# Softmax totals spread through DRAM, and one sequence's layernorm moved into the sequence before

## The chip, the cores and the metric

The kernel runs on one core of one Trainium2 chip. Its time is device microseconds for one execution. All data are float32.

## What is computed

There are four sequences of 1024 tokens with 1024 features. Each passes through a causal attention layer of 32 heads of 32 features, and then through a layer in which each token uses the best of 8 low-rank adapters. Both layers have a layernorm without weights before them and a residual around them.

```
xn   = layernorm(x)                                  # (4, 1024, 1024)
q,k,v = xn @ wq, xn @ wk, xn @ wv                    # 32 heads x 32
q, k = rotary(q), rotary(k)
p    = softmax(causal(q k^T / sqrt(32)))             # per head 1024 x 1024
x    = x + (p v) @ wo
y    = layernorm(x)
gate = one_hot(argmax(y @ route_w^T)) * max(y @ route_w^T)      # of 8
x    = x + ((gate * (y @ A^T)) @ Bw) * scaling       # rank 16 each
```

## The kernel before

**Units.** A unit is one sequence `b` with one group `g` of four heads; there are 32 units, `units[u]`, in order of sequence, so units 0 to 7 are sequence 0. In each unit the kernel scores four heads, exponentiates, and multiplies with the values. Queries come as 16 tiles `t` of 64; a "half" `blk` is eight of these tiles. Beside that, between the scores of unit `u`, a list of steps `between[u]` is worked off: the projections `q`, `k`, `v` for unit `u + 1` (`chain`, 8 matmul steps for each of 6 chains, L302), and from sequence 1 on a part of the *previous* sequence's end: one token tile of `wo` (`project`), its layernorm and transposes (`turn`), the router (`route`), and the adapter (`turn_hidden`, `adapt`).

**The order.** All engines' queues are in the order in which the program text is run; nothing is reordered later. A unit runs through eleven `SLOTS`. Most are score rounds: `score_round` (TensorE, then copies by ScalarE, then the mask by GpSimd at L420), `find_tops` (VectorE's row maxima, L438, and their exchange, L459), some exponentials (ScalarE, L467), whose 32x32 transposes by VectorE (`turn_probabilities`, L492) make them ready for the value matmuls. After each round `fill` works off a share of the steps, by their costs (a projection step is 1.0; steps of cost 0 only put an instruction in its place). The two slots `"second"` and `"first"` call `apply`, which multiplies one half with the values (`value_pieces`, L573, for the second half of unit `u - 1` and the first half of unit `u`), and then scales the result by the reciprocal of the softmax totals (`scale_values`, L593). Until L593 has read it, the bank of the value sums is not free for the next score round.

**The totals.** `join_sums` adds the two halves of the totals (L534), takes the reciprocal on VectorE (L535), and lets GpSimd copy each reciprocal 32 times (L537) into a tile `by` of queries by features. `spread_sums` turns `by` to features by queries with four transposes on TensorE (L547) and one copy by ScalarE (L548). L593 multiplies with it. `join_sums` is called as soon as the last tile of a half has been transposed; `spread_sums` behind the value matmuls.

**Postponed work.** `postponed` holds pairs of a cost and a function. After each step `do_postponed` takes the step's cost off and runs what has come down to zero. It serves the rotary embedding.

**The next sequence's layernorm.** `Norm` does it for a sequence's eight token tiles: `load` (a DMA from `x` to a tile of tag `row`, of which there are five, or to a tile of a not yet used `qT` or `kT`, as `homes` says), `find` (moments, L175 to L181), `scale` (L186), and `turn` (eight transposes on TensorE, L198, and two copies). `after` names the tiles that are loaded when one has been turned. For sequence 1, the loads of tiles 0 to 4 stand at the start of unit 5's steps; two tiles are scaled in unit 5, four in unit 6, and the last two in unit 7. Tiles 0 to 3 can only be turned when the projections of unit 7 have released the old `xnT`, in unit 6; the others are turned in unit 7, by the list that `change_steps` builds. For sequences 2 and 3 `change_steps` also weaves in what the previous sequence has left: `p` (16 `wo` steps), `tail` (`turn`, `route`, `turn_hidden`, `adapt`) and `held`, the last value chain of the unit, as `h[0]` to `h[7]`.

**Streams.** SyncE's queue (SP) issues all DMAs. From sequence 1 on the `wo` and router weights come as chunks in four tiles of tag `chunk` (`load_chunk`, L647); the chunk four places on is loaded when one has been used. The values go through DRAM as well (`vd`, L507 and L513).

Of the kernel before, what the change touches and what calls it, by code (L numbers as in the profile page):

```python
# [14 lines left out]
P = 128  # L15
# [56 lines left out]
def tile_preln_attn_then_top1_lora(  # L72
# [87 lines left out]
    half_sb = const.tile([P, 1], F32, name="half_sb")  # L160
    nc.vector.memset(half_sb, -0.5)
    sign_sb = const.tile([P, 1], F32, name="sign_sb")

    def sign_sines():

# [60 lines left out]
    def do_postponed(cost):  # L226
        for item in list(postponed):
            item[0] -= cost
            if item[0] <= 0:
                postponed.remove(item)  # L230
                item[1]()

    class Norm:

# [8 lines left out]
        def load(self, *tiles):  # L245
            u = self.b * NG
            for t in tiles:
                n = self.homes.get(t)
                if not n:
                    self.x[t] = load_x(self.b, t)  # L250
                    continue
                dsts = qTs if n == "q" else kTs
                if u not in dsts:
                    dsts[u] = big.tile([P, S], F32, tag="qkT", name=f"{n}T_{u}", bufs=4)
                self.x[t] = dsts[u]
                nc.sync.dma_start(dsts[u], x[self.b, t * P : (t + 1) * P, :])
# [7 lines left out]
        def scale(self, t):  # L264
            while self.scaled <= t:
                k = self.scaled
                self.find(k + 1 if self.b == 0 else k)
                normalize(self.x[k], self.x[k], self.moments.pop(k))
                self.scaled += 1
                if self.b == 1:  # L270
                    self.find(k + 1)

        def turn(self, t):
            half, k = divmod(t, TB)
# [250 lines left out]
    def join_sums(u, blk):  # L525


        if (u, blk) in bys or any((u, t) in places for t in range(blk * QT, (blk + 1) * QT)):
            return
        den = dens.pop((u, blk)).rearrange("p (t c) h -> p c t h", c=2)  # L530
        rec = small.tile([P, TB, HG], F32, tag="rec", name=f"rec_{u}_{blk}", bufs=2)
        for i in range(P // SQ):
            rows, other = slice(i * SQ, (i + 1) * SQ), slice((i ^ 1) * SQ, ((i ^ 1) + 1) * SQ)
            nc.vector.tensor_tensor(rec[rows], den[rows, i % 2], den[other, i % 2], ALU.add)  # L534
        nc.vector.reciprocal(rec, rec)  # L535
        bys[u, blk] = by = big.tile([P, TB, P], F32, tag="by", name=f"by_{u}_{blk}")
        nc.gpsimd.tensor_copy(  # L537
            by.rearrange("p t (h d) -> p t h d", d=HD),
            rec.unsqueeze(3).to_broadcast([P, TB, HG, HD]),
        )  # L540

    def spread_sums(u, blk):

        by = bys.pop((u, blk))
        pt = bank([P, TB, P], f"pr_{u}_{blk}")
        for i in range(TB):
            nc.tensor.transpose(pt[:, i, :], by[:, i, :], eye_sb)  # L547
        nc.scalar.copy(by, pt)  # L548
        return by.rearrange("p t k -> p (t k)")

    def value_pieces(u, blk):

# [236 lines left out]
    def change_steps(u, norm, project, tail, held):  # L789
# [7 lines left out]
        if p:  # L797
            turn, route, turn_hidden, adapt = tail
            find = norm.finding
            load_last = Step(lambda: norm.load(7), 0.0)  # L800
            out += [*h[:2], turn, *h[2:4], find(3), p[0], h[4], turning(2), h[5], p[1], route, scaling(3)]
            out += [find(4), h[6], p[2], h[7], p[3], turn_hidden, scaling(4), *p[4:6], adapt, load_last]
            out += [p[6], find(5), p[7], turning(3), scaling(5), *p[8:10], turning(4), *p[10:12]]
            chains = weave(chains[:-6], p[12:]) + chains[-6:]
            out += [*chains[:2], find(6), *chains[2:4], scaling(6), turning(5), *chains[4:6], find(7)]
            out += [*chains[6:8], scaling(7), turning(6), *chains[8:14], turning(7)]
            return out + chains[14:]
        out += [*chains[:2], turning(4), scaling(6), *chains[2:6], turning(5), scaling(7)]
        out += [*chains[6:11], turning(6), *chains[11:16], turning(7)]
        return out + chains[16:]  # L810

    USUAL = (("q", 0), ("k", 0), ("q", 1), ("k", 1), ("v", 0), ("v", 1))
    ENDING = (("q", 0), ("q", 1), ("k", 0), ("v", 0), ("k", 1), ("v", 1))
# [8 lines left out]
    for u, (b, g) in enumerate(units):  # L822
# [13 lines left out]
        if u + 1 < len(units) and g + 1 == NG:  # L836
            last_v = between[-1]
            if b:
                norm = Norm(b + 1, {0: (2,), 2: (5,), 3: (6,)}, {3: "q", 4: "k", 6: "q"})
                load = [Step(lambda norm=norm, t=t: norm.load(t), 0.0) for t in range(2)]  # L840
                for at, step in (
                    (own["k", 0][0], load[0]),
# [9 lines left out]
                ):  # L852
                    behind(last_v, at, step)
            else:
                norm = Norm(b + 1, {0: (5,), 1: (6,), 2: (7,)})
                for t, at in enumerate((("k", 1), ("k", 1), ("k", 1), ("v", 1))):
                    behind(last_v, own[at][(1 + 3 * t) % NC], norm.turning(t))
                behind(last_v, own["v", 1][6], norm.scaling(5))
                behind(last_v, own["v", 1][3], norm.finding(5))
                behind(last_v, own["k", 0][4], norm.scaling(4))  # L860
                behind(last_v, own["q", 1][2], norm.scaling(3))
                behind(last_v, own["q", 0][2], norm.scaling(2))
                for t in (1, 0):
                    between[-2].insert(10 + 16 * t, norm.scaling(t))
                between[-2].insert(0, Step(lambda norm=norm: norm.load(*range(TB + 1)), 0.0))
            steps = change_steps(u + 1, norm, project, tail, held)
            norms[b + 1] = norm
        else:
# [274 lines left out]
```

## Time and profile before

| What | us |
|---|---|
| median of 3 runs (lowest, highest) | 2747.32 (2746.83, 2750.49) |
| the profiled execution: own time | 2747.7 |
| its span | 2745.9 |
| one unit of sequence 0 (unit 3) | 65.3 |
| units 5, 6, 7, in which sequence 1 is normalized | 70.2, 77.5, 72.8 |
| one steady unit of sequences 1 to 3 | 82.3 |
| units 15 and 23, in which the sequence changes later | 97.7 |

A unit is measured here from its first value matmuls for the second half of the unit before it to the same place in the next unit. In the profile, L12 is line 12 of the kernel; PE is TensorE, PEld its weight loads, DVE VectorE, ACT ScalarE, POOL GpSimd, SP SyncE. A group's line gives the busy time, the mean duration of one in ns, and the idle time of that engine just before it with what ended it. A line of the timeline gives start and length in us, engine, line, operation, what is written and read, and in brackets the idle time before. Two records belong to each float32 matmul step of 512 columns.

### The profile page before, as it was taken

The page shows a single profiled execution, that of the slowest core. Times are in us where ns is not written, and L with a number is a line of the kernel's source. Part 1 is how long each engine was busy: PE and PEld are TensorE (multiplying, and loading weights), DVE is VectorE, ACT ScalarE, POOL GpSimd, SP SyncE. Part 2 cuts the span into 40 slices and gives each one's busy share as a digit, 9 for nine tenths or more (in the row PEclk, how much of TensorE's full clock was granted, in tenths as well). Part 3 has the DMA queues.
Part 4 walks back from the last instruction along what each step waited for, and adds up shares of the span by engine and source line. Part 5 has one row for each costly group of instructions (what it writes and reads, how often), then busy time and mean ns, then how long its engine had stood idle before and what let it go on. Part 6 is the DMA issues. An engine that isn't in the chain of part 4 may idle for free.

```text
span 2745.9 us, 84082 instructions
## 1 busy us (share of the span) xinstructions
PE 2682.2 (98%) x35328; PEld 1322.0 (48%) x35328; DVE 2126.7 (77%) x4198; ACT 1755.0 (64%) x5033; POOL 638.1 (23%) x900
## 2 busy tenths in 40 slices
PE   8999999899999999989999999998999999999998
PEld 5444444444445444445444454444544444544445
DVE  4888889887777877887777778788777777778655
ACT  2877777876666676666666666666566666666521
POOL 2222223222222222222222222222222222222000
PEclk9999999999999999999999999999999999999999
DMA  3222232325444455551654444565255544446421
GB/s 118 52 56 56 56 94 56 78 56 150 131 135 114 121 141 142 151 171 43 175 145 122 135 110 121 149 165 146 63 157 150 138 128 128 115 119 196 129 67 55
DMA packets 448012, 317.86 MB, mean 116 GB/s; under 512 B 150289, under 2 KB 371729, under 8 KB 447633
## 3 DMA queue, kind: packets, MB, share of 16 engines
q1 hardware_dynamic: 447632, 312.47, 41.6%
q8 instruction: 278, 4.55, 0.7%
q14 instruction: 102, 0.83, 0.1%
HBM read 262.59 MB, written 49.81 MB: 114 GB/s over the span
## 4 chain that ended last, share of the span: by engine, by line
PE 80%; DVE 14%; ACT 2%; DMA 1%; POOL 1%; issue 1%; SPq 0%; POOLq 0%; DVEq 0%; ACTq 0%
PE po L690 14%; PE pq L313 14%; PE pk L313 13%; PE pv L313 12%; PE s L406 11%; PE av L573 9%; DVE top L438 4%; DVE pr L492 4%; PE ph L712 2%; PE pf L751 2%; DMA chunk<-in_wo 1%; DVE both L459 1%; PE pr L547 1%; ACT pr L417 1%; PE pt_f L198 1%
## 5 line engine op out<-in xcount | busy, mean ns | idle before, releaser
L467 ACT ACTIVATE pr<-pr,both 128x256 f32<-128x256 f32 (+15 forms) x2048 | 1045.1, 519 | 58.0 <-DVE both L459 57.9
L438 DVE TENSOR_REDUCE top<-pr 128x2 f32<-128x960 f32 (+15 forms) x768 | 651.1, 894 | 251.5 <-POOL pr L420 250.9
L417 ACT COPY pr<-s 128x640 f32<-128x640 f32 (+14 forms) x544 | 525.3, 1017 | 492.3 <-PE s L406 491.7
L492 DVE STREAM_TRANSPOSE pr<-pr 128x1024 f32<-128x1024 f32 (+11 forms) x768 | 664.3, 907 | 33.3 <-ACT pr L467 30.1
L420 POOL TENSOR_TENSOR pr<-pr,causal_sb 128x128 f32<-128x128 f32 x512 | 238.0, 472 | 1070.6 <-ACT pr L417 1062.4
L313 PE MATMUL pv<-xnT,wv 128*128 128x512 f32 x1024 | 484.1, 600 | 0.0
L313 PE MATMUL pq<-xnT,wq 128*128 128x512 f32 x1008 | 476.8, 600 | 0.6 <-ACT xnT L200 0.6
L313 PE MATMUL pk<-xnT,wk 128*128 128x512 f32 x1008 | 475.9, 601 | 0.0
L406 PE MATMUL s<-kT,qT 32*32 32x256 f32 (+4 forms) x17408 | 393.0, 385 | 10.7 <-ACT pr L417 7.2
L467 ACT ACTIVATION_READ_ACCUMULATOR pr<-pr,both 128x1 f32 x2048 | 400.8, 196 | 0.0
L690 PE MATMUL po<-chunk,attn 128*128 128x512 f32 x736 | 376.3, 597 | 4.0 <-DMA chunk<-in_wo 4.0
L406 PEld LDWEIGHTS s<-kT,qT 32*32 32x32 f32 x17408 | 187.2, 103 | 267.2 <-issue 101.8
L313 PEld LDWEIGHTS pk<-xnT,wk 128*128 128x128 f32 x1008 | 181.3, 190 | 234.8 <-issue 234.6
L313 PEld LDWEIGHTS pq<-xnT,wq 128*128 128x128 f32 x1008 | 182.6, 191 | 224.0 <-issue 221.8
L313 PEld LDWEIGHTS pv<-xnT,wv 128*128 128x128 f32 x1024 | 185.7, 190 | 217.2 <-issue 212.9
L573 PE MATMUL av<-pr,vals 64*32 64x256 f32 (+3 forms) x12288 | 273.2, 320 | 11.7 <-DVE pr L492 11.6
L573 PEld LDWEIGHTS av<-pr,vals 64*32 64x32 f32 x12288 | 215.5, 106 | 119.9 <-issue 54.5
L459 DVE TENSOR_TENSOR both<-top 32x4 f32<-32x4 f32 (+3 forms) x1152 | 213.4, 185 | 23.7
L690 PEld LDWEIGHTS po<-chunk,attn 128*128 128x128 f32 x736 | 135.2, 190 | 168.0 <-issue 149.6
L548 ACT COPY by<-pr 128x512 f32<-128x512 f32 x64 | 37.5, 586 | 260.5 <-PE pr L547 260.5
L593 DVE TENSOR_TENSOR at<-av,by 128x256 f32<-128x256 f32 x128 | 48.1, 417 | 158.1 <-ACT by L548 158.0
L690 PE MATMUL po<-wo,attn 128*128 128x512 f32 x256 | 116.7, 597 | 0.0
(87 smaller groups left out, 1705.8 us busy)
## 6 DMA issues: line engine op xcount, KB each, us to landing
chunk<-in_wo SPq DMA_DIRECT2D x368, 256.0 KB, 3.6
vals<-vd SPq DMA_DIRECT2D x256, 128.0 KB, 4.5
x<-in_x SPq DMA_DIRECT2D x58, 512.0 KB, 6.0
wq<-in_wq SPq DMA_DIRECT2D x32, 512.0 KB, 4.0
wk<-in_wk SPq DMA_DIRECT2D x32, 512.0 KB, 4.0
wv<-in_wv SPq DMA_DIRECT2D x32, 512.0 KB, 4.2
vd<-vT SPq DMA_DIRECT2D x128, 128.0 KB, 4.8
out_y<-x SPq DMA_DIRECT2D x32, 512.0 KB, 2.8
```

What stands on the lines that cost most here:

```text
L313: nc.tensor.matmul(at["p"], lhsT=wt[:, c, :], rhs=xnTs[b, tb][:, c, :], start=(c == 0), stop=(c == NC - 1),)
L406: nc.tensor.matmul(sc[i * SQ : (i + 1) * SQ, h, at : at + w].rearrange("p (j k) -> p j k", k=SQ), lhsT=of_q[rows, 2 * t + half], rhs=of_k[ ...
L417: nc.scalar.copy(pr[:, :, k0 : k0 + w], sc[:, :, at : at + w])
L420: nc.gpsimd.tensor_tensor(diagonal, diagonal, causal_sb.unsqueeze(1).to_broadcast([P, HG, SQ]), ALU.add)
L438: nc.vector.tensor_reduce(top[:, k, h : h + step], places[u, t][:, h : h + step, :], AX.X, ALU.max, negate=True,)
L459: nc.vector.tensor_tensor(dst[rows], src[rows], src[other], op)
L467: nc.scalar.activation(pr[:, h, :], pr[:, h, :], AF.Exp, bias=tops[u, t][:, h : h + 1], accum_out=dens[u, t // QT][:, t % QT, h : h + 1],)
L492: nc.vector.transpose(pr, pr)
L573: nc.tensor.matmul(avs[half][h * HD : (h + 1) * HD, t0:, :], lhsT=v[rows, j, h * HD : (h + 1) * HD], rhs=rhs, start=(j == 0), stop=(j == n ...
L690: nc.tensor.matmul(st["po"], lhsT=lhsT, rhs=rhs, start=(c == start), stop=(c == stop))
L712: nc.tensor.matmul(ph, lhsT=st["ynT"][:, c, :], rhs=w[:, c - i * RA, :], start=(c == 0), stop=(c == NC - 1),)
L751: nc.tensor.matmul(pf, lhsT=st["whT"], rhs=rhs, start=True, stop=True)
```

## The change

1. `join_sums` no longer uses GpSimd. The reciprocals lie as 16 columns (head by tile) in a constant tile `rec_sb`, are transposed in 32x32 blocks on VectorE, and go to DRAM by four small DMAs (`put`); four more (`get`) read them back, each row of 512 totals to the 32 partitions of its head. In sequence 0 both are issued at once; later `put` and `get` are postponed by costs of 2.0 and 4.0. `spread_sums` issues what is still left and returns `by`; its transposes and its copy are gone.
2. Sequence 1's tiles 0 to 3 are loaded, measured and scaled one per unit in units 1 to 4, tiles 4 and 5 in unit 5, tiles 6 and 7 in unit 6. Tiles 5 and 6 lie in two `chunk` tiles each (`Two` hides that from the readers), and are scaled in two instructions of 512 columns.
3. `change_steps` takes its steps in another order. With a previous sequence to finish, all of `h` comes ahead of the second `wo` step, and tile 6 is loaded in a `row` together with tile 7, behind `adapt`, and no longer in `qT` when tile 3 has been turned. Without one, the tiles are turned after 3, 4, 4 and 4 steps.

```diff
+    rec_sb = const.tile([P, 2, SQ], F32, name="rec_sb")
+    nc.vector.memset(rec_sb, 0.0)
...
+                if n == "chunk":
+                    self.x[t] = Two([])
+                    for cols in (slice(0, HALF), slice(HALF, D)):
+                        part = big.tile([P, HALF], F32, tag="chunk", name=f"x_{self.b}_{t}", bufs=4)
+                        nc.sync.dma_start(part, x[self.b, t * P : (t + 1) * P, cols])
+                        self.x[t].parts.append(part)
+                    continue
...
-                normalize(self.x[k], self.x[k], self.moments.pop(k))
+                moments = self.moments.pop(k)
+                for part in getattr(self.x[k], "parts", [self.x[k]]):
+                    normalize(part, part, moments)
                 self.scaled += 1
-                if self.b == 1:
-                    self.find(k + 1)
...
-        den = dens.pop((u, blk)).rearrange("p (t c) h -> p c t h", c=2)
-        rec = small.tile([P, TB, HG], F32, tag="rec", name=f"rec_{u}_{blk}", bufs=2)
+        den = dens.pop((u, blk)).rearrange("p (t c) h -> p c h t", c=2)
+        rec = rec_sb[:, blk, : HG * TB].rearrange("p (h t) -> p h t", t=TB)
         for i in range(P // SQ):
             rows, other = slice(i * SQ, (i + 1) * SQ), slice((i ^ 1) * SQ, ((i ^ 1) + 1) * SQ)
             nc.vector.tensor_tensor(rec[rows], den[rows, i % 2], den[other, i % 2], ALU.add)
-        nc.vector.reciprocal(rec, rec)
-        bys[u, blk] = by = big.tile([P, TB, P], F32, tag="by", name=f"by_{u}_{blk}")
-        nc.gpsimd.tensor_copy(
-            by.rearrange("p t (h d) -> p t h d", d=HD),
-            rec.unsqueeze(3).to_broadcast([P, TB, HG, HD]),
-        )
+        nc.vector.reciprocal(rec_sb[:, blk, : HG * TB], rec_sb[:, blk, : HG * TB])
+        turned = small.tile([P, SQ], F32, tag="recT", name=f"recT_{u}_{blk}", bufs=2)
+        nc.vector.transpose(turned, rec_sb[:, blk])
+        there = dram.tile([HG * TB, P // SQ, SQ], F32, tag="recs", name=f"recs_{u}_{blk}")
+        by = big.tile([P, TB * P], F32, tag="by", name=f"by_{u}_{blk}")
+
+        def put():
+            for i in range(P // SQ):
+                nc.sync.dma_start(there[:, i], turned[i * SQ : i * SQ + HG * TB])
+
+        def get():
+            for h in range(HG):
+                of_h = there[h * TB : (h + 1) * TB]
+                nc.sync.dma_start(
+                    by[h * HD : (h + 1) * HD],
+                    bass.AP(of_h.tensor, of_h.offset, [[0, HD], [1, TB * P]]),
+                )
+
+        left = [put, get]
+        bys[u, blk] = by, left
+        for cost in (2.0, 4.0) if units[u][0] else (0.0, 0.0):
+            postponed.append([cost, lambda: left and left.pop(0)()])
+        do_postponed(0.0)
...
-        by = bys.pop((u, blk))
-        pt = bank([P, TB, P], f"pr_{u}_{blk}")
-        for i in range(TB):
-            nc.tensor.transpose(pt[:, i, :], by[:, i, :], eye_sb)
-        nc.scalar.copy(by, pt)
-        return by.rearrange("p t k -> p (t k)")
+        by, left = bys.pop((u, blk))
+        while left:
+            left.pop(0)()
+        return by
...
-            load_last = Step(lambda: norm.load(7), 0.0)
-            out += [*h[:2], turn, *h[2:4], find(3), p[0], h[4], turning(2), h[5], p[1], route, scaling(3)]
-            out += [find(4), h[6], p[2], h[7], p[3], turn_hidden, scaling(4), *p[4:6], adapt, load_last]
-            out += [p[6], find(5), p[7], turning(3), scaling(5), *p[8:10], turning(4), *p[10:12]]
+            load_last = Step(lambda: norm.load(6, 7), 0.0)
+            out += [*h[:2], turn, *h[2:4], find(3), *h[4:8], p[0], turning(2), p[1], scaling(3), p[2]]
+            out += [route, find(4), *p[3:5], turn_hidden, scaling(4), p[5], adapt, load_last, p[6]]
+            out += [find(5), p[7], turning(3), scaling(5), *p[8:10], turning(4), *p[10:12]]
             chains = weave(chains[:-6], p[12:]) + chains[-6:]
-            out += [*chains[:2], find(6), *chains[2:4], scaling(6), turning(5), *chains[4:6], find(7)]
-            out += [*chains[6:8], scaling(7), turning(6), *chains[8:14], turning(7)]
+            out += [*chains[:2], find(6), *chains[2:4], turning(5), scaling(6), *chains[4:7], find(7)]
+            out += [*chains[7:9], turning(6), scaling(7), *chains[9:14], turning(7)]
             return out + chains[14:]
-        out += [*chains[:2], turning(4), scaling(6), *chains[2:6], turning(5), scaling(7)]
-        out += [*chains[6:11], turning(6), *chains[11:16], turning(7)]
-        return out + chains[16:]
+        for t, n in zip(range(TB, NT), (3, 4, 4, 4)):
+            out += [*chains[:n], turning(t)]
+            del chains[:n]
+        return out + chains
...
-                norm = Norm(b + 1, {0: (2,), 2: (5,), 3: (6,)}, {3: "q", 4: "k", 6: "q"})
+                norm = Norm(b + 1, {0: (2,), 2: (5,)}, {3: "q", 4: "k"})
...
-                norm = Norm(b + 1, {0: (5,), 1: (6,), 2: (7,)})
+                norm = Norm(b + 1, {0: (7,)}, {5: "chunk", 6: "chunk"})
+                for t, (unit, at) in enumerate(((1, 24), (2, 24), (3, 24), (4, 24), (5, 12), (5, 36))):
+                    steps = between[unit]
+                    for k, step in enumerate((norm.load, norm.find, norm.scale)):
+                        steps.insert(at - 8 + 5 * k, Step(lambda step=step, t=t: step(t), 0.0))
+                for at, step in (
+                    (own["q", 0][0], Step(lambda norm=norm: norm.load(6), 0.0)),
+                    (own["q", 1][0], norm.finding(6)),
+                    (own["q", 1][3], norm.scaling(6)),
+                    (own["v", 1][5], norm.finding(7)),
+                    (own["v", 1][7], norm.scaling(7)),
+                ):
+                    behind(last_v, at, step)
                 for t, at in enumerate((("k", 1), ("k", 1), ("k", 1), ("v", 1))):
                     behind(last_v, own[at][(1 + 3 * t) % NC], norm.turning(t))
-                behind(last_v, own["v", 1][6], norm.scaling(5))
-                behind(last_v, own["v", 1][3], norm.finding(5))
-                behind(last_v, own["k", 0][4], norm.scaling(4))
-                behind(last_v, own["q", 1][2], norm.scaling(3))
-                behind(last_v, own["q", 0][2], norm.scaling(2))
-                for t in (1, 0):
-                    between[-2].insert(10 + 16 * t, norm.scaling(t))
-                between[-2].insert(0, Step(lambda norm=norm: norm.load(*range(TB + 1)), 0.0))
```

More of the change, by code (lines that the diff above doesn't have):

```diff
@@ L231, in do_postponed, with __init__, __getitem__ @@
                 item[1]()
+    class Two:
+        def __init__(self, parts):
+            self.parts = parts
+        def __getitem__(self, key):
+            rows, cols = key
+            k, at = divmod(cols.start, HALF)
+            return self.parts[k][rows, at : at + cols.stop - cols.start]
     class Norm:
```

## The prediction

> **What bounds it now.** I read the busy shares and the chain of waits first, then the stage table, then the spots that the diff touches.
>
> ```profile
> PE 2682.2 (98%) x35328; PEld 1322.0 (48%) x35328; DVE 2126.7 (77%) x4198; ACT 1755.0 (64%) x5033; POOL 638.1 (23%) x900
> PE 80%; DVE 14%; ACT 2%; DMA 1%; POOL 1%; issue 1%; SPq 0%; POOLq 0%; DVEq 0%; ACTq 0%
> ```
>
> TensorE (PE) is nearly always busy and holds most of the chain; VectorE (DVE) holds 14% of it. Where that share lies, the stage table shows for one unit of sequence 1 (first line) and one of sequence 0 (second line; a unit's time runs from the first value matmuls for the second half of the unit before to the same place one unit on; columns: window, length, busy us of PE, weight loads, DVE, ACT, POOL, then clock, DMA share, GB/s):
>
> ```profile
> 1374.55:1456.87 82.32, 82.32 (x1094) 40.04 (x1093) 64.22 (x127) 53.66 (x157) 19.48 (x28) 1.00 0.47 130
> 269.85:335.14 65.29, 64.37 (x1033) 30.61 (x1032) 56.48 (x112) 52.46 (x154) 18.46 (x26) 1.00 0.25 59
> ```
>
> From sequence 1 on PE has no gap in a steady unit, and DVE has 18 us to spare: PE time taken out there shortens the run one to one. In sequence 0 a unit has no `wo` projection; DVE is 56.5 of 65.3 us busy and PE already waits 0.9 us in it. The largest waits of PE:
>
> ```profile
> PE av L573 <- DVE pr L492: 11.6, 2, 9.1
> PE pt_a L198 <- ACT yn L200: 5.2, 2, 2.6
> PE pt_a L198 <- DVE qT L186: 4.5, 2, 2.3
> PE po L690 <- DMA chunk<-in_wo: 4.0, 5, 1.7
> ```
>
> The 9.1 us lie at 539 to 548, in unit 6, where DVE normalizes four tiles of sequence 1; the next two are at the later changes of sequence (1185 and 1229, again 1860 and 1904). The change meets both. Its other part removes these:
>
> ```profile
> L547 PE MATMUL pr<-eye_sb,by 128*128 128x128 f32 x256 | 42.2, 287 | 0.9 <-issue 0.9
> L548 ACT COPY by<-pr 128x512 f32<-128x512 f32 x64 | 37.5, 586 | 260.5 <-PE pr L547 260.5
> L537 POOL COPY by<-rec 128x512 f32<-128x512 f32 x64 | 39.1, 612 | 220.1 <-DVE rec L535 220.1
> ```
>
> **What the Trainium skill says.** "DMA: Bandwidth & Descriptors", Anatomy of one DMA, gives some 2.0 us fixed per DMA, mostly the receipt of the last write. It is fitted on GpSimd's path; here the 256 KB `attn<-at` stores from SP land after 3.4 us and the 128 KB `vals<-vd` loads after 4.5, so 2 us for a few KB is plausible. The same page, Rules for kernel authors, has the issuing engine wait for a first DMA before a second reads what it wrote: each `get` waits on SP for its `put`, as `vals<-vd` does now behind `vd<-vT` (33.2 us of SP waits in 33). "TensorE: Matmul & The Clock Gate", Part 1, halves PE's clock after some 3.4 us idle: after the 9.05 us wait the 128 value matmuls take 5.90 us, elsewhere 3.68.
>
> **The change, part by part.** *PE.* Four transposes stand together 64 times. The timeline of one:
>
> ```profile
> 708.01 0.66 PE L547 MATMUL pr<-eye_sb,by 128*128 128x128 f32 x4
> 708.50 1.02 PE L690 MATMUL po<-chunk,attn 128*128 128x512 f32 x2
> ```
>
> The next matmul starts 0.49 us after them, not 287 ns times four: that is what they hold. 64 x 0.49 = 31.4 us in all. *ACT* loses 64 x 0.586 us and a wait in its queue for PE; it is not the bound. *POOL* loses 64 x 0.61, and one thing on DVE's path:
>
> ```profile
> 303.76 0.61 POOL L537 COPY by<-rec 128x512 f32<-128x512 f32 x1 [5.24 <-DVE rec L535]
> 304.33 0.46 POOL L420 TENSOR_TENSOR pr<-pr,causal_sb 128x128 f32<-128x128 f32 x1
> 304.82 1.09 DVE L438 TENSOR_REDUCE top<-pr 128x2 f32<-128x896 f32 x1 [1.19 <-POOL pr L420]
> ```
>
> The mask addition (its input is there at 301.3) stands behind the copy, which stands behind the reciprocal; DVE idles 1.19 us. That goes, once per unit. *DVE* gains a 128x32 transpose; the 128x128 one takes 0.30 us, I take 0.2 (0.1 to 0.3).
>
> *The way by DRAM.* From the reciprocal's start: 0.25 and 0.2 us on DVE; four stores issued at 0.35 each on SP (`attn<-at` takes 0.33), 1.4; landing 2.0; four loads issued, 1.4; landing 2.1. Sum 7.4 us. Bounds: 5.5, were issue 0.1 each; 14.2 with the landings of `vd<-vT` (4.8) and `vals<-vd` (4.5) and 0.75 per store. By now L593 comes at least 7.9 us after the reciprocal in sequence 0 (first half of the queries), 9.3 there (second half), some 10.8 later, but 3.0 in unit 0. L593 could come 1.3 us sooner where it waits for ACT. In sequence 1, window 9.4: hidden; the `put` and `get` come up to 4 units of cost later in SP's order, still ahead of L593, and the next scores need the bank only 4 us after it. In sequence 0, first half, DVE loses its 1.19 of idle, so the window is 6.7: L593 waits 0.7. In unit 0 it waits about 4.4 us, ahead of a PE wait for DVE (2.6 us at 135) that has no slack.
>
> *SP behind the put.* `put` waits for DVE, `get` for the landing; chunk loads of `wo` and the router stand behind. At the second half of unit 10 SP would be held from about 861 to 868; the chunk issued at 864.1 is used at 875.4, with 7.5 us to spare after landing (3.9 us). Hidden, at some 3 us left. If the way takes 14 us, it is about 1 us late per unit.
>
> *Normalization, sequence 0.* One tile is 2 x 0.68 + 0.21 + 0.15 + 0.81 = 2.53 us of DVE. Before: tiles 0 and 1 in unit 5, four tiles in unit 6, the rest in 7. Now one tile in each of units 1 to 4, two in 5, two in 6, none in 7. The new loads stand 10 us ahead of their use, on an SP that is idle there (x lands in 6.0).
> - Units 1 to 4: PE from the values to tile 15's scores 17.5 - 0.5 = 17.0; ACT and POOL 4.7; DVE from 292.06 to 334.70 with no gap but the 1.19, 42.6 - 1.2 + 2.5 + 0.2 + 0.7 = 44.9; hand-over 0.4. That is 67.1 against 65.3, so +1.8; PE alone would allow -1.9. I take +1.5 each, +6 (from -8 to +10).
> - Unit 0: +4.4 (0 to +6). Unit 5: from 70.2 to some 67.7, -2.5.
> - Unit 6: between 514.6 and 548.6 DVE does three moment findings and two scalings, 7.4 us with a wait for POOL; now one tile, 3.2. L593 comes about 1.8 sooner. The values then start some 6 us earlier, -6; what is late next is still DVE, by some 3 us, so I give no cold clock back.
> - Unit 7: -1.0 on PE, and less DVE: -1.5.
> Sequence 0 together: +4.4 + 6 - 2.5 - 6 - 1.5 = **+0.4**. The cut there is spent on the spread tiles.
>
> *Steady units of sequences 1 to 3* (19 of them, and unit 31): 20 x 0.98 = **-19.6**.
>
> *The two later changes of sequence* (units 14 with 15, and 22 with 23). Tile 6 loaded with tile 7, not after tile 3: the 2.3 us go. Three steps of the held value chain moved ahead of tile 2: the 2.6 us for `yn` go at that place, but DVE is busy, but for 0.7 us, from 1155 to the values at 1194, so PE meets the wait there; DVE itself gains 1.2 from POOL. Half of the transposes, 1.0, count. Loads of tiles 6 and 7 together put one on SP behind the landing of `out_y` (2.8 us), ahead of the chunk that is already 1.6 late: +1.5. So -1.0 - 2.3 - 1.2 + 1.5 = -3.0 each, **-6**. The other moved steps keep their engines' order within a slot; I cost them at nothing, under DVE's queue; uncovered, 1 us.
>
> Sum: -19.6 - 6 + 0.4 = -25.2. The profiled execution took 2747.7 us (span 2745.9), 0.4 above the median of 2747.32: 2747.7 - 25.2 = 2722.5, **2722**.
>
> **The rivals.**
> - *DVE has room in sequence 0 and the boundary waits go whole.* For it: DVE is 87% busy, not 100. Against: it is without a gap from 292 to 335. Units 0 to 7 then give 0 - 4 - 4 - 9 - 3 = -20, the boundaries 2 x -7.3: 2747.7 - 19.6 - 20 - 14.6 = 2693.
> - *Slower: the way by DRAM is longer than its window.* Place: L593 of the first half in sequence 0, in DVE's gapless stretch. Each us above 7.4 costs 8 units 1 us; from 7.4 + 25.2/8 = 10.5 us on the whole gain is lost. At 12 us: -25.2 + 37 = +12, 2760. For it: landings of 4.5 and 4.8 us in this trace; against: those move 128 KB in small pieces, these 64 KB in rows of 2 KB.
> - *Given back in the steady units*: SP held at `put`, a chunk 1 us late in each of 24 units: +24, 2746, no change. Against: the spare 7.5 us.
> - *The DMAs are only issued at L593*, because the postponed steps have not run: would show as 6 us of DVE wait each. Some seven units of cost lie between, so only unit 0 is so; no time of its own.
>
> **How the numbers follow.** The main case has 0.72, 2708 to 2736 by the ends of units 0 to 4; the first rival 0.13; slower 0.09; given back 0.06. The range leaves out some 0.1 above and 0.1 below: 2698 to 2746. A measurement here can tell about 0.2%, 5.5 us: faster 0.85, same 0.06, slower 0.09.
>
> **What would show it.** L547, L548 and L537 gone; steady units 81.3 us with no PE gap; L593 after PE and not after ACT, with waits on a DMA only in unit 0 and the first halves of sequence 0; no 1.19 us ahead of `top` at 304; the 9.05 us wait down to some 3; tile 6's 2.3 gone. Wrong would be: steady units above 82 (chunks late), waits of several us at L593 in every unit, or units 1 to 4 shorter than 64.5 us (then DVE had room).

## The result and the profile after

The change makes the kernel slower: **2779.18 us** median (2775.41 to 2782.6, 4 runs), against 2748.29 (2746.83 to 2750.49, 4 runs) for the kernel before, run beside it. The ratio is 1.0111, with a 95% interval of 1.0094 to 1.0129. The forecast was 2722, in a range of 2698 to 2746. The profiled execution after took 2781.2 us, its span is 2779.4: 33.5 more than before.

The busy shares and the chain of the kernel after:

```profile
PE 2678.8 (96%) x35072; PEld 1305.0 (47%) x35072; DVE 2153.1 (77%) x4265; ACT 1718.6 (62%) x4969; POOL 601.0 (22%) x836
PE 80%; DVE 12%; DMA 3%; ACT 2%; SPq 1%; issue 1%; POOL 1%; POOLq 0%; DVEq 0%; ACTq 0%
```

PE has 256 instructions fewer and is busy 3.4 us less, not 31. The mean granted clock fell from 0.998 to 0.987, and an estimate from that, 1.1% of 2680 us or 29, is about what the transposes gave. DMA, 1% of the chain before, now holds 3%, and SP, which was below 1%, now 1%. The stage table, for a unit of sequence 0 and a steady one (columns as before: length, busy us of PE, weight loads, DVE, ACT and POOL, clock, DMA share, GB/s):

```profile
282.60:352.20 69.60, 64.91 (x1027) 30.39 (x1026) 60.76 (x118) 51.43 (x151) 18.22 (x25) 0.98 0.29 70
1402.80:1484.50 81.70, 81.70 (x1086) 39.38 (x1085) 64.80 (x129) 52.49 (x155) 18.19 (x25) 1.00 0.51 138
```

The steady unit is shorter and still without a PE gap. Unit 3 is 4.3 us longer than before: DVE is busy 60.8 instead of 56.5, and PE now stands 4.7 us instead of 0.9. The largest waits of PE say where else the time is:

```profile
PE s L427 <- DVE at L630: 24.3, 6, 4.9
PE ph L749 <- DMA chunk<-in_ra: 18.9, 2, 9.8
PE pt_a L200 <- DVE x L188: 16.8, 6, 9.5
PE po L727 <- DMA chunk<-in_wo: 8.9, 4, 3.6
PE av L610 <- DVE pr L513: 7.3, 2, 5.5
```

(L427, L630, L749, L727, L610, L188, L200 are the lines 406, 593, 712, 690, 573, 186, 198 of before; columns: total, how often, longest.) The last line is what was hoped for in unit 6, 9.1 down to 5.5. The first was 2.3 us in two waits before; now the scores wait for L630 in each of units 0 to 5. The second is new: two waits of the router, one at each later change of sequence. The longest wait of the third line is the start of the kernel, 9.5 us, where it was 9.1 before.

By stages, with the units of the table above (difference after minus before, us of the profiled spans):

| stage | forecast | profile |
|---|---|---|
| start and unit 0 | +4.4 | +6.8 |
| units 1 to 4 | +6 | +15.3 |
| unit 5 | -2.5 | +3.1 |
| units 6 and 7 | -7.5 | -7.1 |
| the rest of sequences 1 to 3 | -19.6 | -13.1 |
| the two later changes of sequence | -6 | +28.5 |
| sum | -25.2 | +33.5 |

More than half of the miss of 58.7 us, 34.5, lies in four units: 14, 15, 22 and 23.

### The profile page after: what moved, and what is told of

It is laid out like the page before. It is cut to its first block, busy times and chain, and to the rows that moved or that the text cites. A ratio compares the mean times of both kernels' runs of the same rounds, so it can differ in the third digit from the quotient of the medians.

```text
span 2779.4 us, 84025 instructions
## 1 busy us (share of the span) xinstructions
PE 2678.8 (96%) x35072; PEld 1305.0 (47%) x35072; DVE 2153.1 (77%) x4265; ACT 1718.6 (62%) x4969; POOL 601.0 (22%) x836
## 4 chain that ended last, share of the span: by engine, by line
PE 80%; DVE 12%; DMA 3%; ACT 2%; SPq 1%; issue 1%; POOL 1%; POOLq 0%; DVEq 0%; ACTq 0%
PE po L727 14%; PE pq L334 14%; PE pk L334 14%; PE pv L334 12%; PE s L427 11%; PE av L610 9%; DVE top L459 3%; DVE pr L513 3%; PE ph L749 2%; PE pf L788 2%; DMA chunk<-in_wo 1%; DVE both L480 1%; PE pt_f L200 1%; ACT pr L438 1%; DVE st_a L177 1%
## 5 line engine op out<-in xcount | busy, mean ns | idle before, releaser
L334 PE MATMUL pv<-xnT,wv 128*128 128x512 f32 x1024 | 491.3, 608 | 0.0
L427 PE MATMUL s<-kT,qT 32*32 32x256 f32 (+4 forms) x17408 | 398.5, 391 | 29.4 <-DVE at L630 24.3
L727 PE MATMUL po<-chunk,attn 128*128 128x512 f32 x736 | 381.0, 604 | 9.1 <-DMA chunk<-in_wo 8.9
L427 PEld LDWEIGHTS s<-kT,qT 32*32 32x32 f32 x17408 | 188.6, 103 | 289.8 <-issue 138.1
L610 PE MATMUL av<-pr,vals 64*32 64x256 f32 (+3 forms) x12288 | 274.9, 322 | 7.3 <-DVE pr L513 7.3
L610 PEld LDWEIGHTS av<-pr,vals 64*32 64x32 f32 x12288 | 215.1, 107 | 116.0 <-issue 58.3
L727 PEld LDWEIGHTS po<-chunk,attn 128*128 128x128 f32 x736 | 135.6, 190 | 174.5 <-issue 150.8
L630 DVE TENSOR_TENSOR at<-av,by 128x256 f32<-128x256 f32 x128 | 48.3, 419 | 124.1 <-PE av L610 95.3
L727 PE MATMUL po<-wo,attn 128*128 128x512 f32 x256 | 116.8, 597 | 1.1 <-DMA attn<-attn 1.1
L372 POOL TENSOR_TENSOR qT<-qT,swapq 128x512 f32<-128x512 f32 x64 | 81.7, 1276 | 154.6 <-DVE swapq L368 154.6
```

Of the source, the lines that this page charges most:

```text
L334: nc.tensor.matmul(at["p"], lhsT=wt[:, c, :], rhs=xnTs[b, tb][:, c, :], start=(c == 0), stop=(c == NC - 1),)
L372: nc.gpsimd.tensor_tensor(dst[:, cols], dst[:, cols], other, ALU.add)
L427: nc.tensor.matmul(sc[i * SQ : (i + 1) * SQ, h, at : at + w].rearrange("p (j k) -> p j k", k=SQ), lhsT=of_q[rows, 2 * t + half], rhs=of_k[ ...
L610: nc.tensor.matmul(avs[half][h * HD : (h + 1) * HD, t0:, :], lhsT=v[rows, j, h * HD : (h + 1) * HD], rhs=rhs, start=(j == 0), stop=(j == n ...
L727: nc.tensor.matmul(st["po"], lhsT=lhsT, rhs=rhs, start=(c == start), stop=(c == stop))
```

## The experiments

The change has three parts: D (totals through DRAM), N (tiles of sequence 1 spread) and O (new order and common load of tiles 6 and 7 at the later changes of sequence). Runs e1 to e3 take parts away; the others follow each cost to its place. Each ratio is to runs of the kernel before taken beside that run (their medians: 2751.7 for e1 to e4, 2752.5 for e5 to e8, 2750.8 for e9 to e12).

| run | what it is | median us | ratio (95%) | units 1-4 | 14+15 | 22+23 |
|---|---|---|---|---|---|---|
| after | D+N+O | 2779.2 | 1.0111 (1.0094, 1.0129) | +15.3 | +13.5 | +15.1 |
| e1 | D | 2737.9 | 0.9948 (0.9931, 0.9964) | -8.3 | +3.0 | +2.4 |
| e2 | N+O | 2773.4 | 1.0080 (1.0065, 1.0095) | +15.8 | +7.0 | +8.5 |
| e3 | D+N | 2754.2 | 1.0009 (1.0002, 1.0015) | +16.5 | +2.9 | +3.0 |
| e4 | D+N+O, put later | 2768.2 | 1.0057 (1.0042, 1.0072) | +15.6 | +4.2 | +5.9 |
| e5 | D+N, tile early | 2735.4 | 0.9939 (0.9924, 0.9955) | -5.6 | +0.1 | +0.5 |
| e6 | step order of O alone | 2767.5 | 1.0053 (1.0037, 1.0068) | -1.9 | +8.1 | +10.7 |
| e7 | loads of O alone | 2761.0 | 1.0030 (1.0018, 1.0043) | +0.1 | +8.1 | +5.6 |
| e8 | D, put later | 2739.7 | 0.9957 (0.9944, 0.9970) | -6.7 | -0.6 | -2.4 |
| e9 | e5, first half by GpSimd | 2734.2 | 0.9941 (0.9929, 0.9954) | -1.5 | +1.2 | +2.3 |
| e10 | after, tile early | 2758.5 | 1.0024 (1.0014, 1.0034) | -5.6 | +14.1 | +14.1 |
| e11 | e5, scaling late | 2742.7 | 0.9965 (0.9955, 0.9976) | +3.9 | +5.2 | +2.3 |
| e12 | e7, loads apart | 2751.5 | 1.0004 (0.9996, 1.0012) | -0.1 | +2.8 | -0.2 |

The last three columns are differences to before in one profile each. How far one profile can be trusted: D with the old order at the changes of sequence (e1, e3, e5, e9, e11, none with a later put) gives +0.1 to +5.2 there, and units 1 to 4 of e6, where nothing was changed, -1.9. A difference of 3 us at one change says nothing by itself.

**e1, e2, e3: which part.**

```diff
e1: the kernel before, with only join_sums, spread_sums and rec_sb of the change
e2: the changed kernel, with join_sums and spread_sums of before
e3: the changed kernel, with the old step lists in change_steps and tile 6 in qT
```

> The kernel before with only the totals sent through DRAM; normalization and step order as before. Theory A (three separate causes): unit 0 loses some 5 to 7 us because the reciprocal stands right ahead of L593's successor there and the way by DRAM takes 7.5 us; units 1 to 5 stay within 1 us of before (some 1.2 us of waiting for the DMA against the 1.19 us that GpSimd's copy cost); steady units gain 0.78; units 14, 15, 22, 23 gain about 1 each, since the router's chunks are asked for ahead of the put. Sum about 2735 us. Rival B (the DRAM way alone makes sequence 0 slow): units 1 to 5 lose 3 to 5 us each, and the run takes 2755 or more. Rival C (the put on SP alone makes the changes of sequence slow): units 14 and 22 lose some 8 us each also here.

> The changed kernel with the totals spread as before (GpSimd's copy, four transposes on TensorE, ScalarE's copy); spread normalization and the new order of steps kept. Theory A: units 1 to 4 lose some 3 us each for one tile of normalization in VectorE's tight stretch, unit 5 about nothing, unit 6 gains 6 to 8; units 14, 15, 22, 23 within 2 us of before, since no put stands ahead of the router's third chunk. Sum 2745 to 2755 us. Rival B: units 1 to 5 as before, sum near 2738. Rival D (the new order alone starves the router of its third chunk): units 14 and 22 lose some 8 us each here too, sum above 2765.

> The changed kernel with the old order of steps at the two later changes of sequence (and tile 6 in qT again); totals through DRAM and spread normalization kept. Theory A and rival D: the 9 us waits for the router's chunk vanish, units 14 and 15 together are 1 us below the kernel before in place of 13.5 above, and 22 with 23 likewise: about 2779 - 29 = 2750 us. Rival C: units 14 and 22 stay 8 us long, 2775.

D alone is faster than before by 0.5%. Its units 1 to 4 are 8.3 us shorter in sum; units 0 and 5 give 4.5 and 4.7 of that back, and sequence 0 as a whole is 2.7 us shorter. So the way by DRAM is not what slows units 1 to 4, which was the place of the slower rival. Without D, units 1 to 4 are still 15.8 longer, and without O 16.5: it is N. The changes of sequence cost 13 to 15 us only with D and O together; O without D costs 7.0 and 8.5, so theory A of e2, which held the order harmless without the DMAs and gave 2745 to 2755 for its time, was wrong there.

What D frees is seen on DVE at the first L593 of unit 3, in the kernel before:

```profile
279.89 0.76 DVE L593 TENSOR_TENSOR at<-av,by 128x256 f32<-128x256 f32 x2 [2.78 <-ACT by L548]
```

What N fills is the place where the change puts the tile, later in the same unit of the kernel after:

```profile
308.86 0.15 DVE L181 TENSOR_SCALAR ve_a<-mv_a 128x1 f32<-128x1 f32 x1
309.09 0.55 POOL L183 TENSOR_TENSOR rstd_a<-ve_a,half_sb 128x1 f32<-128x1 f32 x1 [4.90 <-DVE ve_a L181]
309.61 1.28 POOL L367 TENSOR_TENSOR qT<-rawq,cos_sb 128x512 f32<-128x512 f32 x1
309.68 1.76 DVE L188 TENSOR_SCALAR x<-x,mv_a,rstd_a 128x1024 f32<-128x1024 f32 x1 [0.66 <-POOL rstd_a L183]
...
328.26 0.76 DVE L630 TENSOR_TENSOR at<-av,by 128x256 f32<-128x256 f32 x2 [1.14 <-DMA by<-recs]
329.17 2.12 PE L427 MATMUL s<-kT,qT 32*32 32x384 f32 x64 [4.34 <-DVE at L630]
```

The first idle time of DVE, 2.78 us, was a wait for ACT's copy of `by`. D ends it: in the kernel after, DVE stands 1.42 us at this place, for PE's values. The change does not use that hole. It puts the tile in the stretch that has none: DVE waits 0.66 us for GpSimd's `rstd`, and the scaling then takes 1.76 us instead of 0.81, beginning 0.07 us after GpSimd's rotary product and ending 0.55 us behind it. The Trainium skill, "SBUF — State Buffer", Who interferes with whom, says that DVE in a two-port mode and GpSimd take turns at a shared pair of ports, for a whole instruction, and the other blocks; the trace agrees: 0.77 us where GpSimd is idle (e5), 1.75 or 1.76 in each of units 1 to 4 here. Everything behind is later: the reciprocal, the way by DRAM that starts with it, and L630 at 328.26, which stands its last 1.14 us for that DMA. PE, which needs that bank, stands 4.34 us. In e2, without the DMAs, it stands 2.7 to 2.8 us at this place in units 1 to 4, and they are as long in sum: the DMA is the last to arrive, but N costs as much without it. The 64 score matmuls behind the wait then take 2.12 us instead of 1.50: the clock has fallen.

**e5 and e11: the place of the tile.**

```diff
-for t, (unit, at) in enumerate(((1, 24), (2, 24), (3, 24), (4, 24), (5, 12), (5, 36))):
+for t, (unit, at) in enumerate(((1, 12), (2, 12), (3, 12), (4, 12), (5, 12), (5, 36))):
```

(e5 is e3 with this line. e11 is e5 with `norm.scale` of units 1 to 4 put at 26 again.)

> The kernel with totals through DRAM, spread tiles and the old step order (run e3: 2754.2 us, units 1 to 4 together 16.5 us longer than before), but with the tile of units 1 to 4 loaded, measured and scaled 12 steps earlier in the unit (places 4, 9 and 14 of the step list in place of 16, 21 and 26). Theory A (it is the place: the scaling stands in VectorE's queue beside GpSimd's rotary product, takes 1.75 us there instead of 0.81 after a wait of 0.66 us, and lies just ahead of the transposes and of the scaling of the values that the next score round waits for): moved off that place, units 1 to 4 come out at most 6 us longer than before together, the wait of the score matmuls for L630 falls from 4.2 to 4.9 us per unit to under 2, and the time is some 2744. Rival B (it is the amount: 2.5 us more for a VectorE without slack, wherever they stand): units 1 to 4 stay 12 to 17 us longer and the time at 2751 to 2755.

> Run e5 with the loads and moments of the tiles in units 1 to 4 at the early places 4 and 9, but the scaling (L188) back at place 26, as in the changed kernel. Theory A (one instruction at the wrong place is most of it: L188 there stands beside GpSimd's rotary product, 1.75 us instead of 0.77, ahead of the transposes and L630 which the next score round waits for): units 1 to 4 are again 5 to 12 us longer in sum than before, against -5.6 in e5, some 2748. Rival B (the amount of work in VectorE's gapless stretch decides): only 4 x 0.8 us = 3.2 us come back, units 1 to 4 at -2.4, some 2739.

e5 moves the same work twelve steps forward; its median is 18.8 us below that of e3. GpSimd and DVE of e5, in unit 3:

```profile
275.30 1.28 POOL L367 TENSOR_TENSOR qT<-rawq,cos_sb 128x512 f32<-128x512 f32 x1
275.39 1.75 DVE L368 TENSOR_TENSOR swapq<-swapq,sin_sb 128x512 f32<-128x512 f32 x1
...
278.22 1.20 DVE L1071 STREAM_TRANSPOSE vT<-vT 128x1024 f32<-128x1024 f32 x1
279.35 0.77 DVE L188 TENSOR_SCALAR x<-x,mv_a,rstd_a 128x1024 f32<-128x1024 f32 x1
280.04 0.74 DVE L630 TENSOR_TENSOR at<-av,by 128x256 f32<-128x256 f32 x2
```

and the stage table for the same unit:

```profile
269.20:333.60 64.40, 63.56 (x1025) 29.86 (x1024) 60.37 (x119) 51.47 (x153) 17.92 (x25) 1.00 0.31 76
```

The scaling sits in the hole before L630, and L630 has no idle time ahead of it. The collision has not gone, it has moved: in each of the four units DVE's own rotary product, L368, now takes 1.75 us beside GpSimd's instead of 0.69, and L630 is still not late. DVE is as busy as in the kernel after, 60.4 us, in a unit 5.2 us shorter. So it is not the amount, and not a collision by itself; it is what waits behind the place.

e11 answers for the scaling alone. At place 26 of that kernel it misses GpSimd's product (0.81 us, no wait for `rstd`, in all four units), and still 9.5 us come back over four units, 2.4 us for each instruction of 0.81. That is more than rival B's 0.8, less than theory A's 5 to 12 above before. Units 1 to 4 of e5, e11 and e3 (columns as before):

```profile
139.42:399.10 259.68, 255.25 (x4097) 119.63 (x4097) 242.74 (x476) 205.05 (x603) 72.05 (x100) 1.00 0.31 75
140.89:410.03 269.14, 255.16 (x4097) 119.61 (x4097) 245.63 (x476) 205.53 (x603) 71.75 (x100) 1.00 0.29 73
140.11:421.85 281.74, 264.09 (x4097) 123.04 (x4097) 245.13 (x476) 205.92 (x604) 72.77 (x100) 0.96 0.29 71
```

All of e11's 9.5 us is idle time of PE, 14.0 us instead of 4.4, mostly in two waits per unit (1.67 and 1.80 in unit 3), and the clock stays at 1.00. In e3 PE idles 17.7 us, with one wait of 4.1 to 4.4 in each unit; the clock is 0.96, and the same matmuls take 8.9 us more. Of the 22.1 us between e5 and e3, then, 9.5 belong to the late scaling, and 12.6 to the late load, the late moments and the collision together, with which the wait is one long one. How these share the 12.6 was not measured.

**e4 and e10: the changes of sequence, D with O.**

```diff
e4:  -for cost in (2.0, 4.0) if units[u][0] ...    +for cost in (5.0, 7.0) if units[u][0] ...
e10: the changed kernel with the line of e5 alone
```

> The changed kernel with put and get postponed by 5.0 and 7.0 units of cost in place of 2.0 and 4.0 from sequence 1 on, so that the third router chunk is asked for ahead of the put at the changes of sequence. Theory A: the 9 us wait of TensorE for the router's chunk in units 14 and 22 falls below 2 us, and units 14 and 22 come to 82 to 84 us; the way by DRAM still ends ahead of L593 at the second halves, and a little late at the first halves (waits of 1 us or less on VectorE, which has room): about 2760 us. Rival D: the waits stay, 2778.

> The changed kernel (2779.2 us) with one edit: the tiles of units 1 to 4 are loaded, measured and scaled at places 4, 9 and 14 of the unit's steps instead of 16, 21 and 26. Theory A (the place of the tile and the cost at the changes of sequence add up): units 1 to 4 fall from +15.3 to about -5 us against before, the changes of sequence stay at +13 to +15 each, and the time is 2757 to 2760. Rival B (the two costs are one, by a state of VectorE or SP that unit 8 and later inherit): the changes of sequence shrink too, below +8 each, 2745 or less.

SP and PE of the kernel after, at the first of the two changes:

```profile
1201.27 0.38 SPq L684 DMA_DIRECT2D chunk<-in_ra  x1
1210.42 1.72 SPq L565 DMA_DIRECT2D recs<-recT  x4
1212.24 0.37 SPq L127 DMA_DIRECT2D x<-in_x  x1
1212.70 0.39 SPq L684 DMA_DIRECT2D chunk<-in_ra  x1
...
1205.67 1.66 PE L749 MATMUL ph<-chunk,yn 128*128 128x136 f32 x12 [1.84 <-ACT vT L352]
1216.38 1.27 PE L749 MATMUL ph<-chunk,yn 128*128 128x136 f32 x4 [9.05 <-DMA chunk<-in_ra]
1217.58 5.00 PE L610 MATMUL av<-pr,vals 64*32 64x256 f32 x128
```

In the kernel before, the first `wo` step at the change runs at 1180.5, and SP asks for the last router chunk at 1181.54, 8 us ahead of the router at 1189.4. In the new order that step comes behind the whole held value chain, at 1200.2. Unit 14 starts 15.3 us later in this kernel, so within the unit that is 4.4 us later; and since three `wo` steps now stand ahead of the router instead of two, the last router chunk is asked for only when the second of them has run. Two router chunks are then asked for late: one at 1201.27, and the next stands on SP behind `put`, which waits until DVE has transposed `recT` at 1210.4. PE waits 9.05 us, and the values behind it take 5.00 us for what takes 2.35 at full clock. With `put` later (e4) the chunk is asked for at 1201.22 and SP issues `put` at 1207.85:

```profile
1205.41 0.73 PE L749 MATMUL ph<-chunk,yn 128*128 128x136 f32 x4 [0.66 <-DMA chunk<-in_ra]
1206.07 4.14 PE L610 MATMUL av<-pr,vals 64*32 64x256 f32 x128
```

Units 14 and 22 come out 1.6 and 0.5 us below before, instead of 8.2 and 8.7 above, and the two changes together give back 9.3 and 9.2 us: that much is `put` ahead of the chunk. Still the time is 2768.2, not theory A's 2760. The last unit is 7.2 us longer: L630 waits 4.18 us there for the postponed loads, `yn` stands behind it on DVE, and PE waits 4.4 us for `yn`. And units 15 and 23 stay 5.8 and 6.3 longer, about what the common load costs there by itself (e7, below). e10 shows that N and the changes of sequence are separate costs: units 1 to 4 fall to -5.6, the changes stay at +14.1 each, and 2758.5 lies in the 2757 to 2760 that theory A gave.

**e6, e7, e12: what O costs without D.**

```diff
e6:  the kernel before, new step lists, load_last still norm.load(7), tile 6 still in qT
e7:  -load_last = Step(lambda: norm.load(7), 0.0)        +... norm.load(6, 7) ...   (tile 6 no longer in qT)
e12: e7 with norm.load(6) at load_last and norm.load(7) behind p[7]
```

> The kernel before, with only the new order of the steps in change_steps for the two later changes of sequence; tile 6 still goes to the free qT after tile 3, and only tile 7 is loaded behind adapt. Run e2 put the cost of the order and the loads together at 7.0 and 8.5 us in units 14 with 15 and 22 with 23. Theory A (the second load of x, which stands behind the landing of out_y on SP ahead of the chunks, is what costs): the two changes are within 2 us of before, the time within 4 us of it. Rival B (the order costs: the wo and router chunks are used, so released and reloaded, later): +5 to +8 us at each change, some 2760.

> The kernel before with its old step order, but with tile 6 of sequences 2 and 3 loaded in a row together with tile 7, behind adapt. Theory A (the load behind the landing of out_y costs): the wait of PE for the wo chunk after the change grows from 1.6 us to 4 to 6, each change is 4 to 8 us longer, some 2760. Rival B (the order costs, not the loads): each change within 2 us of before, or up to 2 us shorter because the wait for tile 6 in qT (2.3 us) goes.

> Run e7 (the kernel before with tile 6 of sequences 2 and 3 in a row; 8.1 and 5.6 us longer at the two changes of sequence) with the two loads apart: tile 6 behind adapt, tile 7 two steps of the wo projection later. Theory A (SP waits 2.0 us at the second load for the landing of out_y, with four wo chunks behind it; the late chunk makes PE wait 3.3 to 4.9 us and its clock then falls): the chunk's wait goes back to 1.5 to 2 us and each change to within 3 us of before, some 2752. Rival B (it is having the row's load there at all, 512 KB ahead of the chunks on the same rings): as in e7, +5 to +8 each, 2760.

e6 settles nothing. Its order turns tile 6 behind the rotary product that writes the next queries to the same `qT`, so what is turned as tile 6 are queries, and PE has a wait that neither kernel has, once at each change (here the first):

```profile
PE pt_a L198 <- POOL qT L346: 4.9, 1, 4.9
```

e7 and e12 are clean. SP and PE in e7, then SP in e12:

```profile
1212.00 0.34 SPq L755 DMA_DIRECT2D out_y<-x  x1
1212.40 2.81 SPq L127 DMA_DIRECT2D x<-in_x  x2
1215.31 2.96 SPq L647 DMA_DIRECT2D chunk<-in_wo  x4
1219.84 3.78 PE L690 MATMUL po<-chunk,attn 128*128 128x512 f32 x4 [3.33 <-DMA chunk<-in_wo]
```

```profile
1209.40 0.34 SPq L755 DMA_DIRECT2D out_y<-x  x1
1209.79 0.42 SPq L127 DMA_DIRECT2D x<-in_x  x1
1210.33 1.27 SPq L647 DMA_DIRECT2D chunk<-in_wo  x2
1212.38 0.33 SPq L127 DMA_DIRECT2D x<-in_x  x1
```

In e7 the second load takes the row that `out_y` is still being stored from, and SP stands 2.0 us for that landing with four `wo` chunks behind it. PE waits 3.33 us for a chunk instead of 1.57 (4.89 instead of 1.73 at the other change), and the next four matmuls take 3.78 us instead of 1.98. Units 15 and 23 are 5.5 and 5.8 us longer for it; the other 2.6 us of the first change lie in unit 14, ahead of these loads, and are taken up in the last section. Two steps apart, the second load finds `out_y` landed, the chunk's wait is back at 1.64 and the time at that of before. The same sequence stands in e2 (SP holds the pair of loads for 2.87 us, PE waits 3.87 and 5.93). e2 less e7 leaves -1.1 and +2.8 us for the new step order with N, within the scatter.

**e8 and e9: towards the best.**

```diff
e8: e1 with    for cost in (5.0, 7.0) if units[u][0] and u < len(units) - 1 else (0.0, 0.0):
e9: e5 with the join_sums and spread_sums of before for (u, blk) == (0, 0)
```

> Totals through DRAM alone (run e1: 2737.9 us), with put and get postponed by costs of 5.0 and 7.0 in place of 2.0 and 4.0, except in the last unit. Theory A (at the changes of sequence the put stands on SP ahead of the wo chunks and makes PE wait 2.6 to 3.0 us for the first of them, and the cold clock after it costs as much again): that wait falls under 1 us, units 14 with 15 and 22 with 23 come out at or below before instead of 2.4 to 3.0 us longer, and the time is some 2732. Rival B (the gets then land too late for L611 or stand themselves ahead of chunks): waits of L611 on a DMA in the steady units, units above 81.5 us, 2740 or more.

> Run e5 (2735.4 us) with the totals of the first half of unit 0 alone spread as in the kernel before, by GpSimd, four transposes and ScalarE's copy: there L630 waits 6 to 7.6 us for the loads from DRAM, since the values follow at once. Theory A: unit 0 is back within 0.7 us of its 29.6 us before, instead of 3.9 longer, nothing else changes, and the time is some 2731 to 2732. Rival B: the 3.9 us are not the wait but the later start of everything behind it, and come back in unit 1: 2735.

e8 brings the changes of sequence below before, as theory A said, but the last unit again pays 6.9 us, though its own `put` was left as it was. The totals of the second half of unit 30 are still postponed, and are needed in unit 31, where L611 stands for their loads (in e1 it has no wait there):

```profile
2549.96 0.76 DVE L611 TENSOR_TENSOR at<-av,by 128x256 f32<-128x256 f32 x2 [3.93 <-DMA by<-recs]
```

The sum is about e1's time, and not the 2732 of theory A. e9 brings unit 0 to -0.3 as expected, but unit 4 and unit 31 are 2.6 and 1.7 longer than in e5 in its profile, and 2734.2 is not distinguishable from 2735.4. **e5 and e9 beat both kernels**: 0.6% below before, and some 44 us below the changed one.

## Why the prediction failed, step by step

Two steps made most of the miss. The new order at the later changes of sequence was costed "at nothing", and SP was taken to hide the `put` there as in a steady unit: the changes cost +28.5 us instead of -6, with waits of 9.05 and 9.82 us for a router chunk behind `put`. And a tile in VectorE's gapless stretch was costed by its length: units 1 to 4 cost +15.3 instead of +6, with a wait of 4.2 to 4.6 us for L630 in each. One by one:

- *The transposes of PE*, mechanism right, size off. Each four hold 0.49 us as read, but the first 512-column matmul behind the values takes 0.10 more in their place: 1.12 instead of 1.02. Before and after:

```profile
1465.54 0.66 PE L547 MATMUL pr<-eye_sb,by 128*128 128x128 f32 x4
1466.04 1.02 PE L690 MATMUL po<-chunk,attn 128*128 128x512 f32 x2
```

```profile
1490.90 2.35 PE L610 MATMUL av<-pr,vals 64*32 64x256 f32 x128
1493.18 1.12 PE L727 MATMUL po<-chunk,attn 128*128 128x512 f32 x2
```

  So 0.78 per unit instead of 0.98: steady units are 81.55, not 81.3.
- *The way by DRAM*, right: 7.4 us forecast. From the reciprocal to the last landing it took 7.5 to 8.1 us in the first halves of units 0 to 4 (6.5 to 6.8 in e1), with four issues in 1.7 us at the least. L630 waits 1.0 to 1.4 us for it in units 1 to 4, against 0.7. The rival of DMAs issued only at L630 is false: `put` goes out 0.03 us after `recT` in sequence 0.
- *Unit 0*, +4.4 forecast and +6.8 found, of which 1.6 lies ahead of the first value matmuls. L630 comes 8.1 us behind the reciprocal there instead of 3.0: 5.1 later, against 4.4.
- *Units 1 to 4*, the term "one tile is 2.53 us of DVE, in a stretch without a gap, +1.5 per unit". It cost 3.8, and 6.2 when D's own gain is taken off (e3 less e1). The sum took the scaling at 0.81 and no wait for `rstd`, and missed the 1.76 and the 0.66. It also set DVE's time against PE's for the whole unit. What decides is the next consumer, L630 and the scores' bank behind it; and PE pays the wait again in clock. e5 shows that the same 2.5 us can cost almost nothing: its units 1 to 4 are 2.7 us longer than those of e1 in sum.
- *Unit 5*, -2.5 forecast and +3.1 found. D alone has +4.7 there, N and O without D +0.5, so it goes with D. PE idles 5.5 us in this unit, 7.3 in e1 and 4.0 before; in both kernels with D some 1.6 us of that stand inside a score round, for nothing that the profile shows ("issue"), where before has 1.3 us of the same kind in unit 2. Why it falls here was not tried, and the cause of unit 5 stays open.
- *Units 6 and 7*: -7.5 forecast, -7.1 found, the wait 5.5 instead of "some 3". The sum came out right in part by luck: most of it was put down to the spread tiles, and they give -3.7 by themselves (e2), D the other -3.7 (e1).
- *The later changes of sequence.* Several steps failed. "The other moved steps ... I cost them at nothing": the steps that moved carry the loads of the router's chunks, which are asked for when a chunk has been used, and the last of these now hangs on the second `wo` step, just ahead of the router. "SP behind the put: hidden" was worked out for a steady unit alone, and holds there (no PE gap in units 9 to 13); at the change the put is ahead of a chunk with nothing to spare. And of the common load, +1.5 was forecast: PE waits 1.8 and 3.2 us more for the chunk in e7, and with the slower matmuls behind it units 15 and 23 are 5.5 and 5.8 longer. The 2.3 us for tile 6 did not go either: e7 still waits 2.19 and the kernel after 1.33 and 1.98, for the scaling on DVE.
- *The rivals.* "DVE has room in sequence 0" was nearer to the truth for D than the main case: -8.3 in units 1 to 4. "Given back in the steady units" is false, since these have no PE gap. The slower rival named the wrong place, and none had the router's chunk behind `put`.

## What to carry to other kernels

Where an engine is 87% busy, ask where its idle time lies, and what waits behind the place, before putting more work on it: twelve steps earlier, in a hole, the same tile cost 5.5 us per unit less. When steps are reordered, follow the loads that their completion triggers, and read what stands ahead of them on the issuing queue at that place, not in a steady stage. A wait of TensorE of 3 us or more should be priced with the slow stretch behind it, and two short waits can be cheaper than one long one (e11 against e3).

## What the hardware showed

A wait of 2.6 us can cool TensorE's clock, and need not. The same transposes after the same wait, in the kernel before and in e7:

```profile
1184.96 1.14 PE L198 MATMUL pt_a<-eye_sb,x 128*128 128x128 f32 x8 [2.60 <-ACT yn L200]
1186.03 1.65 PE L406 MATMUL s<-kT,qT 32*32 32x192 f32 x96
```

```profile
1185.51 1.97 PE L198 MATMUL pt_a<-eye_sb,x 128*128 128x128 f32 x8 [2.58 <-ACT yn L200]
1187.41 2.50 PE L406 MATMUL s<-kT,qT 32*32 32x192 f32 x96
```

In e7 the transposes take 1.97 instead of 1.14 and the scores 2.50 instead of 1.65, and unit 14 is 2.6 us longer with the same gaps. The stage table for it, before and in e7, has the clock in the third column from the end:

```profile
1110.97:1194.12 83.15, 80.55 (x1119) 41.37 (x1118) 70.08 (x140) 57.28 (x165) 20.59 (x31) 1.00 0.61 167
1111.54:1197.28 85.74, 83.16 (x1118) 42.97 (x1117) 72.59 (x148) 57.35 (x165) 21.17 (x32) 0.96 0.58 162
```

The Trainium skill, "TensorE: Matmul & The Clock Gate", Part 1, puts the fall at some 3.4 us of idle, in a window that runs on freely; here 2.58 us was enough once and 2.60 was not. In the clock records of these fourteen traces, between 60 and 2700 us, the clock falls to 0.50 for 3.4, 6.8 or 10.2 us at a time. Every wait of PE of 3.2 us or more had such a stretch at its end; waits of 1.6 to 3.15 us had one or not. An estimate from these lengths: a stretch of 3.4 us costs up to 1.7 us of matmul time, one of 6.8 up to 3.4. That such waits of 2.2 to 3 us stand at each change of sequence, falling on one side or the other, is the likely source of the scatter there; this was not tested.
